# Values instead of keys projected ahead at the boundary between two attention layers, with the softmax inverses one piece later

## The chip, the cores and the metric

The kernel runs on one core of one Trainium2 chip, all in float32. The metric is the device time of one execution in microseconds; the runs shown are given as median, lowest and highest. Profiles are of one execution, with its own time beside them.

## The reference

`x` has shape (8, 512, 32, 32): 8 batch elements, 512 channels, 1024 tokens. Two attention layers follow each other:

```python
# layer 0: layer norm over channels, 8 heads of 64
xn = layer_norm(x_flat, gamma, beta)                 # (B, 1024, 512)
q, k, v = (xn @ W.T + b for W, b in ...)             # heads of 64
attn = softmax(einsum("bqhd,bkhd->bhqk", q, k) / 8)
x = einsum("bhqk,bkhd->bqhd", attn, v) @ Wo.T + bo + x_flat
# layer 1: group norm with 32 groups, one head of 512
h = group_norm(x, gamma, beta)
q, k, v = (einsum("oc,bcn->bon", w, h) + b for w, b in ...)
attn = softmax(einsum("bcn,bcm->bnm", q, k) * 512 ** -0.5)
out = x + wp @ (v attn^T) + bp
```

## The kernel before

**Products.** Nearly all large products (projections, layer 1's scores and values) are done with seven block products instead of eight: both operands are cut in 2 x 2 blocks, sums of blocks (S1 to S4 of the weights, T1 to T4 of the data) are formed beforehand on VectorE, and seven products of blocks are added into four results. The class `Product` does one such product for one *unit*, a half of the output rows or tokens. Its `step` runs over these seven steps:

```python
STEPS = [("11","11","x",True), ("12","21","z",True), ("S2","T2","x",False), ("S1","T1","y",True),
         ("S3","T3","x",False), ("S4","22","y",False), ("22","T4","x",False)]
```

The third entry names the PSUM tile that the step writes; `True` opens it, `False` adds to what is in it. So after the fourth step the content of `y` is copied out (`u(1, 1)`), then the sixth step adds into the same `y`. In the same way `x` is copied out after the first step (`u(0, 0)`) and the third (`u(0, 1)`). `out` (line 347) adds such a copy to a PSUM tile on VectorE. For keys and queries the copy is a ScalarE activation that adds the bias (line 477); for values it is a plain ScalarE copy (line 464); for the output projection it is a VectorE instruction that adds the bias and the residual (line 903).

**Order.** The order of instructions on TensorE, ScalarE, VectorE and GpSimd is the order in which the program is written (`manual_schedule`). DMAs are issued from SyncE (SP) and GpSimd (POOL). Small work that has no fixed place is put into a queue `side` by `later`; `tick` takes one piece from it. A step issues its matmuls, then ticks, then issues its copy or addition:

```python
self.part(getattr(self, to), self.a[a], self.b[b], opens)
tick(self.pieces)
...
elif i == 3:
    self.u4 = self.copy((1, 1), self.y)
```

So what a piece puts on ScalarE or VectorE stands ahead of that step's own copy there.

**One element.** Attention of layer 0 goes over eight pairs of heads and token halves (`Pair`): scores (matmul s, line 807), exponentials on ScalarE (p, line 810), sums over the keys on VectorE (lines 814, 816) and values (acc, line 825). For every two pairs, `PairSums` folds the sums by DMAs, inverts them on VectorE (`invert_folded`, lines 536 to 778), spreads the inverse with eight small ScalarE copies (`copies`, rr, line 871), expands it (`rows`, rden, line 522) and scales the output blocks (`scale`, line 880). Each is a piece of side work. Then come the output projection (x_out, y_out, z_out), the group norm (pm, gn), and layer 1: its combined query-key product (qa), scores (x_s), values projection (vm) and values (x_o).

**Work of the next element.** While the group norm's short chain of small instructions runs, TensorE works on the next element, whose layer norm is ready by then. Before the output projection it does unit 0 of the next element's **keys** (`k_units[0].rest()`), and between the group norm's parts and after them unit 1 (`meanwhile`). The four key tiles of 512 KB are stored to DRAM (`put_away`, k_away) and loaded again (k_again) at the head of the next element. There `next_queries_and_values` projects its queries and then its values, with the layer norm of the element after that running in `side`: its eight copies of the inverse root (line 609) fall into the first unit of the second product. Weights are kept in DRAM and loaded by `load_w` (line 206) through SP, four DMAs for each weight: keys' weights in the second pair of attention, queries' weights after layer 1's values projection, values' weights at the head.

The big buffer pool has 46 tiles of 512 KB, a pool of half tiles 9; PSUM has three tiles of two banks (`ps_s`: x, z, s, acc) and two of one bank (`ps_a`: y, pm).

Of the kernel before, what the change touches and what calls it, by code (L numbers as in the profile page):

```python
# [68 lines left out]
def fast_path(ctx: ExitStack, tc: tile.TileContext, x: bass.AP, vecs: dict, weights: dict, out: bass.AP,  # L69
# [13 lines left out]
    nc = tc.nc  # L83
# [167 lines left out]
    wk_now, wq_now = first_w("k"), first_w("q")  # L251
# [57 lines left out]
    def later(*work):  # L309
        side.extend(work)  # L310
# [169 lines left out]
                           banks_of(tag, r, shared, own))  # L480
        return [unit(r) for r in range(2)], res

    def project_v(tag, w, h):


        res, shared = {}, {}

        def unit(r):
            def dest(i, k):
                if (i, k) not in res:  # L490
                    res[i, k] = big_tile(f"{tag}_{i}{k}")
                return res[i, k][:, ts(r, HB)]

            return Product(f"{tag}_{r}", w, h, token_part(r), plain_shift, dest, banks_of(tag, r, shared))
        return [unit(r) for r in range(2)], res
# [600 lines left out]
    def bias_of(n):  # L1096
        return lambda oc: vec(n, oc)

    with tc.manual_schedule(engines=ORDERED):
# [51 lines left out]
            u.rest()  # L1151
        until(lambda: not side)

        def next_queries_and_values(b, wq, wv, ln):

            units, q = project(f"q{b}", wq, bias_of("bq0"), hb)
            if b == 0:
                ln.xt = load_x(1)
                units[0].step(3)
                ln.queue()  # L1160
            for u in units:
                u.rest()
            units, v = project_v(f"v{b}", wv, hb)
            for u in units:
                u.pieces = 1 if b else 2
            units[0].step(1)
            if ln:
                ln.waiting = False
            for u in units:
                u.rest()  # L1170
            return q, v

        qt, vts = next_queries_and_values(0, wq_now, wv_now, ln)
        for b in range(B):
            more = b + 1 < B
            stats = small.tile([P, NC, NH, 6], F32, tag="stats", name=f"stats_{b}")
            ot = {"tag": f"o_{b}"}
            pairs, groups = [], []

            def next_scores():  # L1180
                i = len(pairs)
                pairs.append(Pair(b, i // NC, i % NC, qt, kt, vts, ot))
                if i % 2 == 0:
                    groups.append(PairSums(f"{b}_{i // 2}", more or i + 2 < HEADS))
                pairs[i].scores(range(NM))
                groups[-1].take(pairs[i])

            for i in range(HEADS):
                if i % 2 == 0:
                    for _ in range(2):  # L1190
                        next_scores()
                p = pairs[i]
                if i < 2 and more:
                    until(lambda: ln.done)
                    later(*(lambda j=j, a=a, i=i: ln.affine(j, i, a) for j in range(2) for a in range(2)))
                if i == 1 and more:
                    wk_next = load_w("k", b + 1)
                if i == 5:
                    wo_now = load_w("o", b)
                if i == 7 and more:  # L1200
                    hb = operands(ln.result())
                    add_operands(hb)
                if i == 7:
                    ob = operands(ot)
                p.values(scaled=(i == HEADS - 1 and not more))
                sums = groups[i // 2]
                if i % 2 == 0 and not sums.folded:
                    sums.product()
                    later(sums.invert, sums.copies, lambda: sums.rows(1), lambda: sums.rows(0), lambda: sums.scale(0))
                elif i % 2 == 1 and sums.folded:  # L1210
                    if i < HEADS // 2:
                        at_scores.append(sums.invert_folded)
                    elif i + 1 < HEADS:
                        later(sums.invert_folded)
                    else:
                        later(lambda: add_operand(ob, "T1"), nothing, sums.invert_folded)
                    later(sums.copies, *(lambda s=sums, f=f, n=n: f(s, n) for f in (PairSums.rows, PairSums.scale)
                                         for n in range(2)))
            o_units, x1 = project_out(b, wo_now, ob, stats)
            if more:  # L1220
                k_units, kn = project(f"k{b + 1}", wk_next, bias_of("bk0"), hb, True)
                k_units[0].rest()
            o_units[0].step(1)
            add_operands(ob)
            o_units[0].step(1)
            o_units[1].step(2)
            o_units[0].rest()
            wa_now = load_w("a", b)
            gn = GroupNorm(b, x1, stats)
            if not more:  # L1230
                until(lambda: not side)
                gn.bank = lambda name: wide_psum(name)[:, :HB]
                for _ in gn.part(slice(0, 1)):
                    o_units[1].step(1)
                t1 = block(f"T1_gn_{b}")
                nc.vector.tensor_sub(t1[:, 0, :], gn.h[0, 1][:, 0, :], gn.h[0, 0][:, 0, :])
            o_units[1].rest()
            wm_now = load_w("m", b)

            def meanwhile(n):  # L1240
                if more:
                    k_units[1].step((2, 1, 2, 2)[n])

            if more:
                until(lambda: not side)
                for n, _ in enumerate(gn.part(slice(None))):
                    meanwhile(n)
            h1 = gn.h
            x1_away = {ik: put_away(wide(t), f"x1_away_{b}_{ik[0]}{ik[1]}") for ik, t in x1.items()}
            h1b = operands(h1)  # L1250
            if more:
                add_operands(h1b)
            a_units, qa = project(f"qa{b}", wa_now, lambda oc: ua[:, oc : oc + 1], h1b,
                                  own="x" if more else "")
            if not more:
                h1b["T1"] = t1
                leads = [(u, i) for i in (0, 1, 3) for u in a_units]
                until(lambda: not side)
                for n, _ in enumerate(gn.part(slice(1, 2))):
                    for u, i in ((leads[:3], leads[3:4], leads[4:])[n]):  # L1260
                        u.lead(i)
                nc.vector.tensor_sub(t1[:, 1, :], h1[0, 1][:, 1, :], h1[0, 0][:, 1, :])
                add_operands(h1b)
            a_units[0].step(1)
            meanwhile(3)
            a_units[0].step(1)
            if more:
                kn_away = {ik: put_away(wide(t), f"k_away_{b + 1}_{ik[0]}{ik[1]}") for ik, t in kn.items()}
            a_units[1].step(2)
            for u in a_units:  # L1270
                u.rest()
            whole = Whole(b, qa, h1b, x1_away)
            s_units = whole.scores()
            whole.query_sums()
            for u in s_units[:2]:
                u.step(2)
            for u in s_units[:2]:
                u.rest()
            whole.key_sums(0)
            whole.operands(0)  # L1280
            for u in s_units[2:]:
                u.rest()
            whole.key_sums(1)
            later(whole.fold)
            whole.operands(1)
            v_units, vm = project_v(f"vm{b}", wm_now, h1b)
            for u in v_units:
                u.rest()
            if more:
                wq_next = load_w("q", b + 1)  # L1290
            o_units = whole.values(vm)
            check = iter(()) if more else all_checks()
            o_units[0].step(1)
            ln = LayerNorm(b + 2) if b + 2 < B else None
            if ln:
                ln.sums()
            whole.inverse()
            o_units[0].step(1)
            next(check, None)
            o_units[1].step(2)  # L1300
            next(check, None)
            o_units[0].rest()
            if ln:
                ln.xt = load_x(b + 2)
                ln.queue()
            o_units[1].rest()
            if more:
                wv_next = load_w("v", b + 1)
                kt = {ik: block(f"k{b + 1}_again_{ik[0]}{ik[1]}") for ik in kn_away}
                for ik, d in kn_away.items():  # L1310
                    nc.sync.dma_start(out=wide(kt[ik]), in_=d)
                qt, vts = next_queries_and_values(b + 1, wq_next, wv_next, ln)


@with_exitstack
# [381 lines left out]
```

## Time and profile before

| what | value |
|---|---|
| median of 3 runs | 2895.97 us (2895.93 to 2896.12) |
| profiled execution, its own time | 2895.56 us |
| its span, first to last instruction | 2893.7 us |
| TensorE matmul busy | 2872.8 us, 99% of the span |
| VectorE, ScalarE, GpSimd busy | 1698.8, 1085.0, 345.2 us |
| DMA | 277.17 MB, mean 96 GB/s |
| granted TensorE clock | 0.999 of full |
| one element, from one y_k wait to the next | 353.5 us |

A row of a timeline gives the start, the duration, the engine (PE is TensorE, PEld its weight loads, ACT ScalarE, DVE VectorE, POOL GpSimd), the line of the kernel, the operation, out<-in by the program's names, and in brackets how long the engine was idle before and what it waited for. The ends of matmuls are modelled, so distances between starts are the safer measure.

### The profile page before, as it was taken

Reading aid. Unit: us, or ns where it says so; the run is one execution under the profiler, and the core shown is the slowest. Engines: PE = TensorE matmul, PEld = TensorE weight load, DVE = VectorE, ACT = ScalarE, POOL = GpSimd, SP = SyncE. Lnnn points to the kernel's source line nnn. Section 1 sums busy time; section 2 is a strip of 40 time slices with the busy share of each in tenths; the row PEclk is TensorE's granted clock in tenths of the full one; section 3 lists DMA queues with packets and bytes.
Section 4 is the critical chain, followed back from the end, with each engine's and each line's share of the span. In section 5 each row is a group of like instructions: output and inputs, shape, how many; then the busy total and the mean of one; then the engine's idle time right before and its main releaser. Section 6 shows DMA issues by size and latency. Waiting matters only on the chain.

```text
span 2893.7 us, 27315 instructions
## 1 busy us (share of the span) xinstructions
PE 2872.8 (99%) x9695; PEld 1386.3 (48%) x9695; DVE 1698.8 (59%) x2181; ACT 1085.0 (37%) x1867; POOL 345.2 (12%) x507
## 2 busy tenths in 40 slices
PE   9999999999999999999999999999999999999999
PEld 4534455345553454534545345543455434553345
DVE  6667354774557645575456755568455674527734
ACT  4462224612256122651226512264222732226321
POOL 2020011200112011120111201011010110002000
PEclk9999999999999999999999999999999999999999
DMA  8134152341613326133252323423244231402302
GB/s 321 41 71 143 33 162 72 69 141 39 182 45 73 135 54 172 44 73 131 64 162 50 87 112 77 149 69 76 104 109 142 62 97 63 124 30 61 118 8 67
DMA packets 110129, 277.17 MB, mean 96 GB/s; under 512 B 16304, under 2 KB 20704, under 8 KB 109984
## 3 DMA queue, kind: packets, MB, share of 16 engines
q1 hardware_dynamic: 81760, 204.51, 20.2%
q0 software_dynamic: 28128, 70.81, 13.2%
q8 instruction: 78, 1.28, 0.2%
q14 instruction: 67, 0.55, 0.1%
q10 hardware_dynamic: 96, 0.02, 0.0%
HBM read 168.85 MB, written 59.24 MB: 79 GB/s over the span
## 4 chain that ended last, share of the span: by engine, by line
PE 90%; DVE 6%; ACT 1%; issue 1%; DMA 1%; DVEq 0%; POOL 0%; ACTq 0%; SPq 0%; POOLq 0%
PE s L807 12%; PE acc L825 12%; PE x_s L451 8%; PE x_o L459 7%; PE x_v L443 4%; PE x_vm L443 4%; PE x_q L434 4%; PE x_qa L434 4%; PE y_o L459 4%; PE y_s L451 4%; PE x_out L434 4%; DVE sum L816 3%; PE x_k L434 3%; PE y_v L443 2%; PE y_vm L443 2%; PE y_out L434 2%
## 5 line engine op out<-in xcount | busy, mean ns | idle before, releaser
L816 DVE TENSOR_TENSOR sum<-sum,p 128x1024 f32<-128x1024 f32 x384 | 470.4, 1225 | 40.1 <-ACT p L810 1.8
L810 ACT ACTIVATE p<-s 128x1024 f32<-128x1024 f32 (+1 forms) x608 | 478.9, 990 | 15.2 <-PE s L807 15.1
L825 PE MATMUL acc<-p,v 128*64 128x512 f32 x2048 | 446.7, 594 | 0.0
L807 PE MATMUL s<-q,k_again 64*128 64x512 f32 x1792 | 392.2, 592 | 0.0
L825 PEld LDWEIGHTS acc<-p,v 128*64 128x64 f32 x2048 | 144.1, 137 | 298.6 <-issue 272.4
L807 PEld LDWEIGHTS s<-q,k_again 64*128 64x128 f32 x1792 | 170.5, 186 | 217.9 <-issue 135.7
L532 POOL DMA_DIRECT2D sum<-sum x78 | 64.2, 823 | 1729.0 <-DVE sum L970 993.9
L528 POOL DMA_DIRECT2D fold<-sum x312 | 208.3, 754 | 327.2 <-DMA sum<-sum 198.0
L814 DVE TENSOR_TENSOR sum<-p,p 128x1024 f32<-128x1024 f32 x64 | 78.2, 1222 | 192.9 <-ACT p L810 192.9
L451 PE MATMUL x_s<-S_qa,T_gn 128*128 128x512 f32 x256 | 120.3, 592 | 0.0
L829 ACT COPY o<-acc 128x512 f32<-128x512 f32 x63 | 36.9, 585 | 220.3 <-PE acc L825 220.1
L459 PE MATMUL x_o<-T_p,S_vm 128*128 128x512 f32 x256 | 115.2, 592 | 0.0
L347 DVE TENSOR_TENSOR p<-u(1, 1)_s,x_s 128x512 f32<-128x512 f32 x32 | 22.0, 688 | 128.6 <-PE x_s L451 128.6
L443 PE MATMUL x_vm<-w_m,T_gn 128*128 128x256 f32 x384 | 90.7, 379 | 0.0
L434 PE MATMUL x_qa<-T_gn,w_a 128*128 128x512 f32 x192 | 89.4, 594 | 0.8 <-ACT qa L477 0.8
L434 PE MATMUL x_out<-T_o,w_o 128*128 128x512 f32 x192 | 89.2, 594 | 0.0
L945 ACT ACTIVATE p<-p 128x512 f32<-128x512 f32 x96 | 60.3, 628 | 60.3 <-DVE p L347 60.3
L477 ACT ACTIVATE u(0, 0)_k<-x_k,vecs 128x512 f32<-128x512 f32 x16 | 11.0, 687 | 187.1 <-PE x_k L434 187.1
L434 PE MATMUL x_k<-T_h,w_k 128*128 128x512 f32 x168 | 79.5, 596 | 0.0
L443 PE MATMUL x_v<-w_v,T_h 128*128 128x256 f32 x336 | 79.4, 379 | 0.0
L434 PE MATMUL x_q<-T_h,w_q 128*128 128x512 f32 x168 | 78.9, 592 | 0.0
L871 ACT COPY rr<-r 32x16 f32<-32x16 f32 x256 | 52.7, 206 | 69.1 <-DVE r L774 65.8
(334 smaller groups left out, 4252.6 us busy)
## 6 DMA issues: line engine op xcount, KB each, us to landing
sum<-sum POOLq DMA_DIRECT2D x78, 256.0 KB, 3.4
fold<-sum POOLq DMA_DIRECT2D x312, 64.0 KB, 2.4
x<-in_x_dram SPq DMA_DIRECT2D x32, 512.0 KB, 9.5
xr<-in_x_dram SPq DMA_DIRECT2D x64, 256.0 KB, 2.7
x_away<-x SPq DMA_DIRECT2D x32, 512.0 KB
x1r<-x_away SPq DMA_DIRECT2D x63, 256.0 KB, 3.1
k_away<-k SPq DMA_DIRECT2D x28, 512.0 KB, 2.6
k_again<-k_away SPq DMA_DIRECT2D x28, 512.0 KB, 6.1
```

The lines of the kernel that those rows point to most:

```text
L434: nc.tensor.matmul(dst, a[:, k, ts(r, P)], b[:, k, :], start=(opens and k == 0), stop=(k == 1), skip_group_check=True)
L443: nc.tensor.matmul(dst[:, ts(m, CB)], b[:, k, ts(2 * r + m, P)], a[:, k, :], start=(opens and m == 0 and k == 0), stop=(k == 1), skip_grou ...
L451: nc.tensor.matmul(dst, b[:, k, ts(r, P)], a[:, k, :], start=(opens and k == 0), stop=(k == 1), skip_group_check=True)
L459: nc.tensor.matmul(dst, a[:, m, ts(r, P)], b[m // 2][:, m % 2, :], start=(opens and m == 0), stop=(m == NM // 2 - 1), skip_group_check=True)
L528: nc.gpsimd.dma_start(out=f[ts(q + i, BL), :], in_=t[ts(n, BL), ts(i, HB)], accum_op=ALU.add if n else ALU.bypass)
L532: nc.gpsimd.dma_start(out=t[:D, :], in_=t[D:, :], accum_op=ALU.add)
L807: nc.tensor.matmul(parts[i], self.k[m // 4][r, ts(m % 4, P)], self.q[r, :], start=True, stop=True)
L810: nc.scalar.activation(dst, src, AF.Exp, scale=1.0 / float(D) ** 0.5)
L814: nc.vector.tensor_add(self.sum, self.p[0], p)
L816: nc.vector.tensor_add(self.sum, self.sum, p)
L825: nc.tensor.matmul(acc[i * D : (i + 1) * D, :], value_of(self.vt, m, self.c * P + i * D, D), self.p[m][:, ts(i, HB)], start=(m == 0), stop ...
L945: nc.scalar.activation(p, s, AF.Exp, scale=float(C) ** -0.5)
```

## The change

It swaps what is projected ahead at the boundary. The next element's values take the place of its keys there: their weights are loaded in the second pair, both units run at the keys' places, each unit with PSUM tiles of its own (`apart=True`), and the four value tiles are stored to DRAM and loaded again at the head. At the head, the keys are projected where the queries were, and the queries where the values were. The function for the two products at the head becomes a general one, called for the first element with queries and values as before. Besides, one more empty piece (`nothing`) stands ahead of the last inversion of an element's sums.

```diff
-    def project_v(tag, w, h):
-        res, shared = {}, {}
+    def project_v(tag, w, h, apart=False):
+        res, shared = {}, None if apart else {}
...
-        def next_queries_and_values(b, wq, wv, ln):
-            units, q = project(f"q{b}", wq, bias_of("bq0"), hb)
-            if b == 0:
+        def two_products(first, second, ln, pieces):
+            units, res = first
+            if ln and not ln.folded:
                 ln.xt = load_x(1)
                 units[0].step(3)
                 ln.queue()
             for u in units:
                 u.rest()
-            units, v = project_v(f"v{b}", wv, hb)
+            units, res2 = second()
             for u in units:
-                u.pieces = 1 if b else 2
+                u.pieces = pieces
             units[0].step(1)
             if ln:
                 ln.waiting = False
             for u in units:
                 u.rest()
-            return q, v
+            return res, res2
...
                 if i == 1 and more:
-                    wk_next = load_w("k", b + 1)
+                    wv_next = load_w("v", b + 1)
...
-                        later(lambda: add_operand(ob, "T1"), nothing, sums.invert_folded)
+                        later(lambda: add_operand(ob, "T1"), nothing, nothing, sums.invert_folded)
...
             if more:
-                k_units, kn = project(f"k{b + 1}", wk_next, bias_of("bk0"), hb, True)
-                k_units[0].rest()
+                n_units, vn = project_v(f"v{b + 1}", wv_next, hb, True)
+                n_units[0].rest()
...
-                    k_units[1].step((2, 1, 2, 2)[n])
+                    n_units[1].step((2, 1, 2, 2)[n])
...
-                kn_away = {ik: put_away(wide(t), f"k_away_{b + 1}_{ik[0]}{ik[1]}") for ik, t in kn.items()}
+                vn_away = {ik: put_away(t, f"v_away_{b + 1}_{ik[0]}{ik[1]}") for ik, t in vn.items()}
...
             if more:
-                wq_next = load_w("q", b + 1)
+                wk_next = load_w("k", b + 1)
...
-                wv_next = load_w("v", b + 1)
-                kt = {ik: block(f"k{b + 1}_again_{ik[0]}{ik[1]}") for ik in kn_away}
-                for ik, d in kn_away.items():
-                    nc.sync.dma_start(out=wide(kt[ik]), in_=d)
-                qt, vts = next_queries_and_values(b + 1, wq_next, wv_next, ln)
+                wq_next = load_w("q", b + 1)
+                vts = {ik: big_tile(f"v{b + 1}_again_{ik[0]}{ik[1]}") for ik in vn_away}
+                for ik, d in vn_away.items():
+                    nc.sync.dma_start(out=vts[ik], in_=d)
+                kt, qt = two_products(project(f"k{b + 1}", wk_next, bias_of("bk0"), hb),
+                                      lambda: project(f"q{b + 1}", wq_next, bias_of("bq0"), hb), ln, 1)
```

More of the change, by code (lines that the diff above doesn't have):

```diff
@@ L1170, in next_queries_and_values @@
                 u.rest()
-            return q, v
-        qt, vts = next_queries_and_values(0, wq_now, wv_now, ln)
+            return res, res2
+        qt, vts = two_products(project("q0", wq_now, bias_of("bq0"), hb), lambda: project_v("v0", wv_now, hb), ln, 2)
         for b in range(B):
```

## The prediction

> **What bounds the kernel now.** I read the page's first part, then TensorE's waits, then the timeline of every engine around the longest of them.
>
> ```profile
> span 2893.7 us, 27315 instructions
> ...
> PE 2872.8 (99%) x9695; PEld 1386.3 (48%) x9695; DVE 1698.8 (59%) x2181; ACT 1085.0 (37%) x1867; POOL 345.2 (12%) x507
> ```
>
> TensorE has 2893.7 - 2872.8 = 20.9 us without a matmul in flight; no other engine is above 59%. The change adds and removes no matmul, so it can only win from the gaps between matmuls, or open new ones. The waits of TensorE:
>
> ```profile
> PE y_k L434 <- ACT u(1, 1)_k L477: 5.1, 7, 0.7
> PE pst_q L263 <- DMA w_q<-in_L_conv_wq_dram: 5.0, 2, 4.7
> PE x_qa L434 <- ACT qa L477: 0.8, 1, 0.8
> ```
>
> Columns: total us, count, longest. Only the first repeats: seven times, once for each boundary between two elements' work (b = 0 to 6). The rest is the start-up or occurs once. The timeline of TensorE at one such boundary (start, duration, what):
>
> ```profile
> 1300.88 1.88 PE L434 MATMUL y_k<-T_h,w_k 128*128 128x512 f32 x4
> 1302.60 1.88 PE L434 MATMUL x_k<-T_h,w_k 128*128 128x512 f32 x4
> 1305.20 1.98 PE L434 MATMUL y_k<-x,w_k 128*128 128x512 f32 x4 [0.72 <-ACT u(1, 1)_k L477]
> 1307.02 1.88 PE L434 MATMUL x_k<-T_h,w_k 128*128 128x512 f32 x4
> 1308.74 1.88 PE L434 MATMUL x_out<-o,w_o 128*128 128x512 f32 x4
> ```
>
> Each row is one of the seven steps of a block product. Steps without trouble start 1.72 us apart (1302.60 - 1300.88; 1308.74 - 1307.02). The sixth step starts 2.60 us after the fifth, and the next 1.82 us after that: 0.88 + 0.10 = 0.98 us lost, of which the waits view shows 0.72. ScalarE at the same place:
>
> ```profile
> 1302.73 1.71 ACT L871 COPY rr<-r 32x16 f32<-32x16 f32 x8 [0.96 <-DVE r L774]
> 1304.46 0.69 ACT L477 ACTIVATE u(1, 1)_k<-y_k,vecs 128x512 f32<-128x512 f32 x1
> ```
>
> y_k's fourth step ended at 1302.60, so its eviction u(1, 1)_k could have run at about 1302.80 (other evictions start 0.20 after their step). It stood behind eight small copies of the softmax's inverse, 1.71 us, and ended at 1305.15. The sixth step accumulates into the same bank, so it waits.
>
> [...] the eviction starts 0.02 us after the eighth copy, and nothing passes it. [...] So I take gaps from starts of matmuls, not from the 99%. [...] where the wait also held the weight load, 0.10 us more is lost on the next step.
>
> **Part 1: inverses one piece later.** The queue of side work holds T1 of o, an empty piece, the inversion, the copies, two expansions (rows), two scalings; each step of the product takes one, after its matmuls are issued and before its eviction. Before, the copies fall on the fourth step, ahead of u(1, 1). One more empty piece puts the inversion there and the copies on the fifth step. The built program shows this: ScalarE's order is now u(0, 1), u(1, 1), then the eight copies. u(1, 1) would run from 1302.80 to about 1303.39 and the sixth step is due at 1304.32: 0.93 us of room. Worth 7 x 0.98 = **-6.9 us**.
>
> What is late next: VectorE's inversion (1300.93 to 1302.86) keeps its time, for nothing stands before it. The copies run 1303.39 to 1305.10 instead of 1302.73 to 1304.44. VectorE then has out(1, 1) at 1304.5, rows 1305.1, out(0, 1) 1306.2, rows 1306.8, the first scaling 1307.4, x_out's addition 1309.7, the second scaling 1310.3, z_out's 1311.4, T2 of o 1312.0 to 1313.2 (0.7 for each 512-wide piece, 1.2 for a 1024-wide one, each addition 0.2 after its step). T2 is wanted by the first unit's third output step, due at 1314.62 (1315.61 now, less 0.98): 1.4 us of room, where T2 now starts at 1311.33 and has 3.0. T4 pushes the eviction of that third step to 1317.4; the fifth step of that unit, which accumulates on it, is due at 1318.05: 0.6 us of room. The loads of xr wait for buffers freed by these pieces, but the latest is freed near 1308 and takes 2.7 us. Cost 0.
>
> **Part 2: values at the boundary, keys beside queries.** Per element this moves 112 matmuls of 256 columns (2 units x 7 steps x 8) from the head of the next element to the boundary, and 56 of 512 columns the other way; a v step is 1.73 us (1513.61, 1515.34), a k step 1.72: sum 0. Eight ScalarE evictions each way (0.58 and 0.69): sum 0. DMAs: four 512 KB stores and four loads are v tiles instead of k tiles, at the same places of SP's queue; the twelve loads of these weights keep their places (v, k, q instead of k, q, v), and POOL's DMAs theirs. The reload is wanted by the first acc rather than the first s, 13.9 us later, so its cover grows. The v tiles are released later than k's were, but the built program's buffer assignments show each load taking a buffer last read as early as before. Cost 0; uncovered, a reload is 6.1 us each.
>
> Two things are not in the trace. The first v step after acc and after the group norm's small matmuls: k loses about 0.20 at each of these three places (first two matmuls 0.10 late each, or 0.11 and 0.08). With 256 columns I take the same; bounds half and one and a half times that, so ±0.1 x 3 x 7 = ±2.1 in all. The other is the queries' eviction in the second product, whose first unit has eight copies of the layer norm's rstd ahead of u(1, 1):
>
> ```profile
> 1518.99 0.58 ACT L464 COPY u(0, 1)_v<-x_v 128x512 f32<-128x512 f32 x1 [2.42 <-PE x_v L443]
> 1519.47 1.70 ACT L609 COPY lnrstdr<-lnr 32x16 f32<-32x16 f32 x8
> 1521.19 0.59 ACT L464 COPY u(1, 1)_v<-y_v 128x512 f32<-128x512 f32 x1
> ```
>
> The row for the sixth v step starts at 1522.24, so 0.46 us are left. For q both evictions are 0.10 longer and the step is due 0.05 earlier: about 0.2 left. That covers the matmul, but the weight load that runs ahead (0.19 us) may be held. Between 0 and 0.15 for each of six elements; I take 0.05: **+0.3 us**.
>
> Sum -6.9 + 0.3 = -6.6. The profiled execution took 2895.56 (span 2893.7 and 1.9 around it), 0.4 below the median 2895.97. It becomes 2889.0, and the median **2889.3**. About 0.2% (5.8 us) is what a measurement of this kernel can tell from no change.
>
> **The rivals.**
> A, the wait goes and nothing takes its place: 2889.3, own range 2887.8 to 2891.0. For it: seven equal waits with one cause, and room at each successor. 0.80.
>
> B, the later scaling chain becomes the wait. If VectorE's work slips one product step (1.72) beyond what I place, the 0.6 us of room at the output's fifth step is gone and 1.1 x 7 = 7.8 us come back: 2897.1. Half a step costs 0.3 x 7 = 1.8: 2891.1. Against it: VectorE has idle gaps of 0.4 to 1.0 us from 1317.5 on. 0.12.
>
> C, slower: the rstd copies become the bound at q's sixth step. Their input is ready at 1518.50, 1.0 before they start. Two product steps (3.4 us) of delay in the layer norm's chain would make six waits of 3.4 - 1.0 - 0.2 = 2.2 us, 13.2 in all: 2902.5. It decides for slower than before from a delay of about 2.4. Against it: fold_var's last DMA is issued by 1508.1, 4.6 us before VectorE's transpose at 1512.70, and the keys' product ahead is the same seven steps per unit as the queries' was. 0.05.
>
> D, the change doesn't do what it says: the copies remain ahead of u(1, 1) in effect, 2896.0. The order on ScalarE speaks against it. 0.03.
>
> **How the numbers follow.** The likeliest is A: 2889.3. A lies mostly beyond the 0.2% line (2890.2), its upper end not; B and D lie within 0.2%. So faster 0.77, same 0.18, slower 0.05. The range leaves out C, D and the worse half of B: 2887.8 to 2891.8.
>
> **What would show it.** Right: no y_v row in TensorE's waits; the copies start after u(1, 1)_v; the sixth step 1.73 after the fifth; elements 352.6 us apart instead of 353.5. Part 1 fails if x_out waits for VectorE's x or T_o in the output projection; part 2 if y_q waits for u(1, 1)_q, or v steps after the group norm's matmuls start over 0.3 late. I am wrong altogether if the span stays above 2891.

## The result, and the profile after

The changed kernel takes 2888.22 us (2887.54 to 2889.69, 10 runs) where the kernel before, run beside it, takes 2895.95 (2894.81 to 2896.18, 10 runs): ratio 0.9975, 95% interval 0.9965 to 0.9984. That is 7.7 us less, by the interval 4.6 to 10.1. Run once more, with its own runs of before, it was 2888.58 against 2895.63, 7.05 us less. The forecast was 2889.3, so 6.6 less than 2895.97.

The profiled execution took 2889.16 us; its page begins:

```profile
span 2887.4 us, 27282 instructions
...
PE 2870.4 (99%) x9695; PEld 1386.7 (48%) x9695; DVE 1698.0 (59%) x2181; ACT 1084.2 (38%) x1867; POOL 345.2 (12%) x507
```

The instructions of TensorE, VectorE, ScalarE and GpSimd are as many as before; only their order changed. The span is 6.3 us shorter than the 2893.7 of before. TensorE's waits, first rows (total, count, longest):

```profile
PE pst_q L263 <- DMA w_q<-in_L_conv_wq_dram: 5.0, 2, 4.7
PE pst_k L263 <- DMA w_k<-in_L_conv_wk_dram: 1.2, 1, 1.2
PE x_qa L434 <- ACT gn L767: 0.8, 1, 0.8
```

The row of seven waits for u(1, 1) is gone, and no row that occurs seven or six times has come in its place. The wait for w_k at the start is 1.2 us here and was 0.6 in the profiled execution before; the changed kernel run again has 0.6, and the profiles of this study have 0.2 to 1.2, so it doesn't come from the change. It makes up 0.6 of the 0.7 us by which the 6.3 us between these two profiles fall short of 7. A measure free of the start-up is the distance from one element's fourth step at the boundary to the next one's, by the starts of matmuls: 353.52 or 353.53 us before, 352.53 now (once 352.97, with a wait of layer 1's x_o that occurs once).

TensorE at the boundary that the prediction showed, now with values (start, duration):

```profile
1298.78 1.89 PE L443 MATMUL y_v<-w_v,T_h 128*128 128x256 f32 x8
1300.51 1.89 PE L443 MATMUL x_v<-w_v,T_h 128*128 128x256 f32 x8
1302.23 1.89 PE L443 MATMUL y_v<-w_v,x 128*128 128x256 f32 x8
1303.96 1.89 PE L443 MATMUL x_v<-w_v,T_h 128*128 128x256 f32 x8
1305.69 1.88 PE L434 MATMUL x_out<-o,w_o 128*128 128x512 f32 x4
```

The sixth step starts 1.72 us after the fifth (2.60 before), the seventh 1.73 after the sixth (1.82 before). ScalarE's timeline there tells why:

```profile
1300.71 0.58 ACT L464 COPY u(1, 1)_v<-y_v 128x512 f32<-128x512 f32 x1 [1.14 <-PE y_v L443]
1301.32 1.70 ACT L871 COPY rr<-r 32x16 f32<-32x16 f32 x8
```

The eviction starts 0.20 us after its step, ahead of the copies, and ends 0.94 us before the sixth step. The place that becomes tight next is T2 of o; VectorE's and TensorE's rows of it:

```profile
1309.92 1.22 DVE L509 TENSOR_TENSOR T_o<-o,T_o 128x1024 f32<-128x1024 f32 x1
...
1311.72 1.22 DVE L509 TENSOR_TENSOR T_o<-o,o 128x1024 f32<-128x1024 f32 x1
```

```profile
1312.55 1.88 PE L434 MATMUL x_out<-T_o,w_o 128*128 128x512 f32 x4
```

T2 (the first row) ends at 1311.14, the step that reads it is due at 1312.55: 1.4 us are left.

### The profile page after: what moved, and what is told of

Same layout as the page of the kernel before. It is cut to its first block, busy times and chain, and to the rows that moved or that the text cites. A ratio compares the mean times of both kernels' runs of the same rounds, so it can differ in the third digit from the quotient of the medians.

```text
span 2887.4 us, 27282 instructions
## 1 busy us (share of the span) xinstructions
PE 2870.4 (99%) x9695; PEld 1386.7 (48%) x9695; DVE 1698.0 (59%) x2181; ACT 1084.2 (38%) x1867; POOL 345.2 (12%) x507
## 4 chain that ended last, share of the span: by engine, by line
PE 99%; DMA 0%; DVE 0%; ACT 0%; issue 0%; SPq 0%; DVEq 0%
PE s L807 15%; PE acc L825 15%; PE x_s L451 8%; PE x_o L459 7%; PE x_v L443 4%; PE x_vm L443 4%; PE x_q L434 4%; PE x_k L434 4%; PE y_s L451 4%; PE x_qa L434 4%; PE x_out L434 4%; PE y_o L459 4%; PE y_v L443 2%; PE y_vm L443 2%; PE y_out L434 2%; PE z_s L451 2%
## 5 line engine op out<-in xcount | busy, mean ns | idle before, releaser
L807 PE MATMUL s<-q,k 64*128 64x512 f32 x2048 | 448.1, 592 | 0.0
L825 PE MATMUL acc<-p,v_again 128*64 128x512 f32 x1792 | 390.9, 594 | 0.0
L807 PEld LDWEIGHTS s<-q,k 64*128 64x128 f32 x2048 | 195.1, 186 | 251.6 <-issue 158.4
L825 PEld LDWEIGHTS acc<-p,v_again 128*64 128x64 f32 x1792 | 126.1, 137 | 261.3 <-issue 238.4
L464 ACT COPY u(0, 0)_v<-x_v 128x512 f32<-128x512 f32 x16 | 9.4, 585 | 187.5 <-PE x_v L443 187.5
L451 PEld LDWEIGHTS x_s<-S_qa,T_gn 128*128 128x128 f32 x256 | 48.6, 190 | 61.2 <-issue 61.0
```

The costliest lines, as they stand in the source:

```text
L451: nc.tensor.matmul(dst, b[:, k, ts(r, P)], a[:, k, :], start=(opens and k == 0), stop=(k == 1), skip_group_check=True)
L807: nc.tensor.matmul(parts[i], self.k[m // 4][r, ts(m % 4, P)], self.q[r, :], start=True, stop=True)
L825: nc.tensor.matmul(acc[i * D : (i + 1) * D, :], value_of(self.vt, m, self.c * P + i * D, D), self.p[m][:, ts(i, HB)], start=(m == 0), stop ...
```

## The experiments

The theory: the whole gain comes from the order on ScalarE, eight small copies ahead of one eviction, and the swap of values and keys moves work without a price or a gain. The rival: the swap brings some or all of it. Times of before are those of the same chip: 2895.35 us (2894.57 to 2896.34) for the first four kernels, 2895.63 (2894.43 to 2896.47) for the last three.

**The extra piece alone.** On the kernel before:

```diff
-                        later(lambda: add_operand(ob, "T1"), nothing, sums.invert_folded)
+                        later(lambda: add_operand(ob, "T1"), nothing, nothing, sums.invert_folded)
```

> The kernel before with one thing changed: one more empty piece ahead of the last inversion. Keys are still projected at the boundary. Theory (the wait is all there is, and only the place of the eight copies in ScalarE's queue makes it): the eviction of y_k runs before the copies, the y_k row leaves TensorE's waits, and the time falls by 7 x 0.98 = 6.9 us to about 2889.1, as with the whole change. Rival (the gain comes from the swap of values and keys, through their cheaper eviction or the later need of the reloaded tiles): within 1 us of before, 2895 to 2896.

Measured: 2888.21 us (2887.79 to 2888.91), ratio 0.9976 (0.9966 to 0.9985). ScalarE in this kernel:

```profile
1300.18 0.69 ACT L477 ACTIVATE u(1, 1)_k<-y_k,vecs 128x512 f32<-128x512 f32 x1 [1.03 <-PE y_k L434]
1300.77 1.69 ACT L871 COPY rr<-r 32x16 f32<-32x16 f32 x8
```

With keys still at the boundary the order is the new one, and so are the time and the distance between elements, 352.53 us (once 352.55). One line of the change carries its gain.

**The swap alone.** On the changed kernel:

```diff
-                        later(lambda: add_operand(ob, "T1"), nothing, nothing, sums.invert_folded)
+                        later(lambda: add_operand(ob, "T1"), nothing, sums.invert_folded)
```

> The changed kernel with the inversion put back one piece earlier; values at the boundary, keys beside the queries. Theory: the eight copies stand ahead of y_v's eviction as they did ahead of y_k's; that eviction is a plain copy of 0.58 us instead of 0.69, so the wait is 0.10 us shorter: 7 x 0.10 = 0.7 us, about 2895.2, with a y_v row of about 4.4 us in TensorE's waits. Rival (the swap brings the gain): 2888 to 2889 and no such row.

Measured: 2894.14 us (2893.69 to 2894.94), ratio 0.9997 (0.9988 to 1.0005), which can't be told from no change, nor from the 2895.2 expected. The waits view and ScalarE's timeline of this kernel:

```profile
PE y_v L443 <- ACT u(1, 1)_v L464: 4.3, 7, 0.9
```

```profile
1302.17 1.71 ACT L871 COPY rr<-r 32x16 f32<-32x16 f32 x8 [1.03 <-DVE r L774]
1303.90 0.58 ACT L464 COPY u(1, 1)_v<-y_v 128x512 f32<-128x512 f32 x1
```

The copies go as soon as VectorE has r, ahead of the eviction. TensorE's wait is back, 4.3 us instead of 5.1, mainly since the plain copy is 0.11 us shorter: by the starts of matmuls 0.84 us are lost at six boundaries instead of 0.99. At the fifth 1.2 are lost, where the copies came 0.37 us later. The swap doesn't remove the wait.

**Only the copies later.** The inversion keeps its piece, the empty piece comes after it. On the kernel before:

```diff
-                        later(lambda: add_operand(ob, "T1"), nothing, sums.invert_folded)
+                        later(lambda: add_operand(ob, "T1"), nothing, sums.invert_folded, nothing)
```

> The kernel before with the second empty piece put between the inversion and the copies, instead of ahead of the inversion: the inversion on VectorE keeps its piece, only what follows it (copies, expansions, scalings) comes one piece later. Keys at the boundary. Theory (ScalarE's copies are the cause, the inversion on VectorE plays no part): the same as one more piece ahead of the inversion, about 2889.1. Rival (the inversion ahead of VectorE's additions of k is part of the loss, so it has to move too): less than the full gain, 2890 to 2895.

Measured: 2888.6 us (2887.59 to 2889.0), ratio 0.9975 (0.9966 to 0.9985): the full gain. It's what ScalarE has ahead of the eviction, not the inversion on VectorE. (The expansions and scalings on VectorE, which follow the copies, moved with them here; that such copies make a wait by themselves is shown by the doubled ones below.)

**One more piece.** On the changed kernel, a third empty piece:

```diff
-                        later(lambda: add_operand(ob, "T1"), nothing, nothing, sums.invert_folded)
+                        later(lambda: add_operand(ob, "T1"), nothing, nothing, nothing, sums.invert_folded)
```

> The changed kernel with yet another empty piece, three in all, so that inversion, copies, expansions and scalings each come one step later still. Theory (the room that is left sits at T2 of o before the third output step): T2 would start only after the second unit's first output addition, near 1311.7 on the changed kernel's clock, and end near 1312.95, where the third output step is due at 1312.55; with the restart 0.5 us at each of seven boundaries, 3.6 us: about 2892 with a row of x_out waiting for T_o on VectorE. Rival (VectorE has the room, nothing shows): the changed kernel's 2888 to 2889. Rival (the fifth output step waits too, 1.1 us each as the prediction's case B has it): 2896 or more.

Measured: 2892.17 us (2891.31 to 2892.98), ratio 0.9989 (0.9982 to 0.9995), 3.6 to 4.0 us above the two kernels with the full gain that ran beside it. Its waits view, VectorE's T2 and TensorE around it:

```profile
PE x_out L434 <- DVE T_o L509: 1.8, 7, 0.3
```

```profile
1312.73 1.22 DVE L509 TENSOR_TENSOR T_o<-o,T_o 128x1024 f32<-128x1024 f32 x1
```

```profile
1311.86 1.88 PE L434 MATMUL z_out<-o,w_o 128*128 128x512 f32 x4
1314.00 1.98 PE L434 MATMUL x_out<-T_o,w_o 128*128 128x512 f32 x4 [0.26 <-DVE T_o L509]
1315.82 1.88 PE L434 MATMUL y_out<-T_o,w_o 128*128 128x512 f32 x4
1317.54 1.88 PE L434 MATMUL x_out<-T_o,w_o 128*128 128x512 f32 x4
```

T2 ends at 1313.95 where the step was due at 1313.58: 0.42 us lost, 0.10 on the next step, 3.7 in seven boundaries. The step two further on starts 1.72 after its predecessor: the third step waits, the fifth does not. So of the three places tried for the copies, one step apart, only the middle one, that of the changed kernel, costs nothing.

**The rstd copies twice.** On the changed kernel, in `spread`, each of these eight copies is issued twice:

```diff
-            for j in range(4):
+            for j in [j for _ in range(2 if name == "rstd" else 1) for j in range(4)]:
```

> The changed kernel with the eight copies of the layer norm's rstd issued twice (the same values written again), in the first unit of the queries' product beside the keys; six elements have them. This prices the prediction's case C. Theory ([...] there is 0.25 us of room at q's sixth step): 1.70 us more ahead of u(1, 1)_q, so a wait of 1.45 and 0.10 for the restart at six places, 9.3 us: about 2897.5, with a y_q row of about 7 us in TensorE's waits. Rival (small copies pass or hide, as the 16 copies are only 3.4 us of ScalarE in a stage where it is busy for a third): no change, 2888.

Measured: 2899.36 us (2898.93 to 2899.98), ratio 1.0013 (1.0006 to 1.0019): slower than the kernel before, and 10.8 above the changed kernel run beside it. The waits view, then ScalarE, then TensorE:

```profile
PE y_q L434 <- ACT u(1, 1)_q L477: 9.2, 6, 1.5
```

```profile
1521.42 3.58 ACT L609 COPY lnrstdr<-lnr 32x16 f32<-32x16 f32 x16
1525.03 0.69 ACT L477 ACTIVATE u(1, 1)_q<-y_q,vecs 128x512 f32<-128x512 f32 x1
```

```profile
1522.35 1.88 PE L434 MATMUL x_q<-T_h,w_q 128*128 128x512 f32 x4
1525.77 1.98 PE L434 MATMUL y_q<-x,w_q 128*128 128x512 f32 x4 [1.54 <-ACT u(1, 1)_q L477]
```

The same mechanism at another place, and here only ScalarE's copies were added. The waits row was expected at about 7 us and is 9.2. The step is 3.42 us long instead of 1.72, and 0.10 are lost after it: 1.80 x 6 = 10.8, which is what the runs show. Expected were 9.3: sixteen copies took 3.58 us where eight take 1.69, so 1.9 more and not 1.7, and of the room of 0.25 the hand-over from ScalarE to TensorE takes 0.05.

**Half the copies ahead.** On the kernel before, four copies on the fourth step and four on the fifth (`copies` now takes the numbers of the halves that it is to do; three dots stand for code that is as it was):

```diff
-                    later(sums.copies, *(lambda s=sums, ...
+                    if i + 1 < HEADS:
+                        later(sums.copies)
+                    else:
+                        later(*(lambda n=n: sums.copies([n]) for n in range(2)))
+                    later(*(lambda s=sums, ...
```

> The kernel before with the eight copies cut into two pieces of side work: four on the fourth step, ahead of u(1, 1)_k, and four on the fifth. Keys at the boundary, the inversion where it was. Theory: u(1, 1)_k comes 0.86 us earlier than before and ends at 1304.3 on the clock of before, where the sixth step is due at 1304.32, so the matmul waits for next to nothing (0.03), and what is left is the weight load that couldn't run ahead, up to 0.10: 7 x (0.03 to 0.13) = 0.2 to 0.9 us over the kernel with one more piece, 2888.4 to 2889.1. Rival (a held weight load costs a restart and more, or the room needed is a good part of a step): over 2890. Rival (number of copies ahead doesn't matter): 2895.

Measured: 2890.09 us (2888.98 to 2890.86), ratio 0.9981 (0.9974 to 0.9989); 1.5 above the changed kernel run beside it, where 0.2 to 0.9 was expected. The theory's range is missed, and the rival's "over 2890" is met by 0.1. ScalarE and TensorE at the same boundary:

```profile
1299.93 0.84 ACT L871 COPY rr<-r 32x16 f32<-32x16 f32 x4 [0.97 <-DVE r L774]
1300.80 0.69 ACT L477 ACTIVATE u(1, 1)_k<-y_k,vecs 128x512 f32<-128x512 f32 x1
1301.51 0.84 ACT L871 COPY rr<-r 32x16 f32<-32x16 f32 x4
```

```profile
1299.79 1.88 PE L434 MATMUL x_k<-T_h,w_k 128*128 128x512 f32 x4
1301.54 1.98 PE L434 MATMUL y_k<-x,w_k 128*128 128x512 f32 x4
1303.36 1.88 PE L434 MATMUL x_k<-T_h,w_k 128*128 128x512 f32 x4
```

The eviction ends at 1301.49 and the sixth step starts 0.03 late, the seventh 0.10 more; the weight load started together with its matmul, at 1301.54. Six of the seven boundaries look like this, 0.8 us together, the upper end of what was expected. At the fifth, near 1654.8, VectorE's inversion and with it the four copies came some 0.65 us later, and the step started 0.67 late, with the same 0.10 after it. That makes 1.6 us in this profile, as much as the runs show, so the miss is the fifth boundary, which the expectation took to be like the others, and not a loss of more than 0.10 after a held load. Why VectorE is late there stays open. This profile is of the fastest of 16 executions; whether the others lose the same at the same places no profile shows.

**The changed kernel again**, beside the last two:

> The changed kernel once more, as the measure for the two runs beside it: about 2888.2, and within 0.5 us of the kernel before with one more empty piece.

Measured: 2888.58 us (2888.0 to 2889.16), ratio 0.9976 (0.9966 to 0.9985). Change, piece alone and copies later alone are within 0.4 us of each other. No version here beats them.

## Why the prediction was right

- **The bound and the loss.** Seven waits at 0.98 us: right, they are 0.99. The starts of matmuls in the profile of before give 0.886 to 0.895 for the late step and 0.104 for the next at each of the seven boundaries, 7.0 in all, and none in the profiles of the changed kernel, the piece alone and the copies later.
- **The sum.** It was -6.6; by the starts of matmuls it is -7.0, the difference being mostly the term of q below. The two measurements gave 7.7 and 7.05. What the first has beyond 7.0 no trace explains; it lies well within its interval.
- **Part 1.** Room for the eviction was put at 0.93 us and is 0.94. VectorE's order and times behind it were as worked out: T2 was placed at 1312.0 on the clock of before, which is 1309.9 on that of after, and started at 1309.92. The 1.4 us of room at T2 are confirmed by the kernel with a third piece, which overdraws them by 0.37 and starts the step 0.42 late.
- **Part 2.** The sum of 0 for the swap was right: with and without it (changed kernel and piece alone) elements are 352.53 us apart. The first v steps after acc and after pm, which no row of before showed, lose the same as k's, 0.10 + 0.10 and 0.11 + 0.08 us; the ±2.1 of that bound weren't needed. The reload of v is waited for nowhere.
- **The term that was mis-sized:** +0.3 for q's sixth step. The room was put at 0.2 us and is 0.25, and the step costs nothing at all: 0. The concern, that the weight load is held, was right; the load just fits. In the changed kernel's profile (first two lines) and with half the copies ahead (last line):

```profile
1519.01 0.39 PEld L434 LDWEIGHTS y_q<-x,w_q 128*128 128x128 f32 x2 [0.47 <-ACT u(1, 1)_q L477]
1519.21 1.88 PE L434 MATMUL y_q<-x,w_q 128*128 128x512 f32 x4
1301.54 0.30 PEld L434 LDWEIGHTS y_k<-x,w_k 128*128 128x128 f32 x2 [0.70 <-ACT u(1, 1)_k L477]
```

In the q steps of this trace a load starts 0.43 us ahead of its matmul where nothing holds it (1518.35 for 1518.78). Here it waited for u(1, 1) and started 0.20 ahead; as it takes 0.19, it was done 0.01 before its matmul was due, at all six elements. With half the copies ahead it started with its matmul, and the next step came 0.10 late. By these numbers a room of less than about 0.24 us (0.05 from the eviction's end to the load, 0.19 for the load) would begin to cost something; that is an estimate, and between the two cases no run here measures. The bounds of the prediction, 0 to 0.15 for each element, cover what came; that it came out at 0 is luck, for 0.01 us decides it.
- **Rival B** named the wrong step. With one step more of delay the wait comes at the third output step, 0.52 us each, not 1.1 at the fifth. The eviction that the fifth step needs is that of the third step; with a third piece T4 no longer stands ahead of it but behind it, so VectorE has done it by 1316.77, where the fifth step starts at 1317.54.
- **Rival C**'s mechanism, copies ahead of q's eviction, exists, as the doubled copies show, and 1.9 us more of them cost 1.8 for each element; its cause (a late layer norm chain) didn't occur. **Rival D** fell with the order on ScalarE.

## What to carry to other kernels

When one engine is busy 99% of the time, look for a small wait that repeats once for each outer iteration, and follow it to what stands ahead of its releaser in that engine's queue; here 1.7 us of tiny copies were worth 0.25% of the kernel. Before moving such a piece later, work out when its last consumer is due, for the window has two ends: one step earlier costs 7 us here, one step later 3.7. In a change with two parts, price them apart: here the larger edit moved tiles, weights and DMAs and gave nothing measurable, the one-word edit gave all. The larger edit also left a place with 0.01 us to spare, q's sixth step, which a next change can overdraw; by the prediction's lines, v had 0.46 us of room there.

## What the runs showed of the hardware

In these traces a step of a block product that waited cost more than its wait: the step after it came 0.10 us late as well, whether the waiting one itself came 1.70 or 0.03 us late (doubled and halved copies). The traces show 0.10 at all 34 places that were read: seven in before, in the swap alone, with the third piece and with the halved copies, six with the doubled ones. At the six places where a weight load was held but done 0.01 us ahead of its matmul (q's sixth step in the changed kernel), none of it is lost: the steps on both sides stay 1.72 us apart. The waits view has none of the 0.10, and since the ends of matmuls are modelled it shows the late start of 0.89 as 0.72: 5.1 us of the 7.0 that could be won.
